# A graph-attention kernel on one core: batches of eight edge tiles in place of four

## The chip, the core and the metric

The kernel runs on one core of a Trainium2 chip. The metric is the device time of one execution in microseconds; the median of three is given. The core has TensorE (PE, its weight loads shown apart as PEld), VectorE (DVE), ScalarE (ACT), GpSimd (POOL) and SyncE (SP), each with an instruction queue of its own that it works off in order. Transfers run on 16 DMA engines; here SP and POOL issue nearly all of them.

## What is computed

One layer of graph attention over 6250 nodes with 128 features (8 heads of 16) and 206250 edges that are sorted by destination, then a residual and a layernorm. Cut to what matters:

```python
Qh, Kh, Vh = (h @ WQ), (h @ WK), (h @ WV)           # reshaped to (N, 8, 16)
Eh = (edge_attr @ WE)                               # (E, 8, 16)
score = einsum('ehd,ehd,ehd->eh', Kh[src], Qh[dst], Eh) / sqrt(16)
score = exp(clip(score, -5.0, 5.0))
msg = Vh[src] * score[:, :, None]
wV = segment_sum(msg, dst); Z = segment_sum(score, dst)
out = layernorm(x + wV / (Z + 1e-06))
```

## The kernel before

Edges are cut into 1612 tiles of 128 (one edge a partition), and tiles into batches of B = 4 (L26; the last eight tiles go in smaller ones, L45 to L53). One pass over the batches does everything.

Ahead of the pass, K and V of all nodes are computed (table, L216) and stored in device memory as kv, 1 KB a node. For each tile, POOL then issues one indirect DMA (gather, L293, issued at L300) that brings the 128 rows of kv that the edges' sources name into kvrows. The first XB = 12 batches don't wait for kv: they gather rows of x and are projected on PE (project, L305). kvrows has GB = 19 buffers of a batch each.

Q[dst] needs no gather, since the edges are sorted. Q's rows are computed 128 nodes at a time, split into three bf16 parts (q_rows, L245) and stored in device memory (qs, L255). For each batch, SP loads the slice qw of QW = 32 nodes, 96 rows (load_q, L258), at an offset read into a register. A transposed one-hot matrix onehotT, made by DVE from relb (each edge's row in the slice, loaded by L274), picks each edge's row in a matmul into the PSUM tile qps (L340). The edge features, loaded as ea in chunks of eight tiles (L284), are projected into the PSUM tile eps (L337). eps and qps have two buffers of one bank each.

The order is written out by hand in the loop at L433. In iteration b:

- loads by SP; the gather of batch b; its matmuls into eps and qps (stage_a, L329)
- DVE's products of batch b-1: kvrows by qps (L346), that by eps (L348), the sum over each head (L351), the clamp (L354) (stage_b)
- DVE's messages of batch b-2 (L382)
- DVE's one-hots of batch b+2, onehot (L322) and onehotT (L326) (stage_0)
- ACT's two exponentials of batch b-1 (weigh, L357)
- PE's sums of batch b-2, onehot by messages, into agg (stage_c, L400)

fill() puts one of the layernorm's 16 small DVE instructions between those. Finished blocks of 128 nodes are added up on PE (finish, L373), normalized and stored by SP. At the end of an iteration Q's rows for later batches are computed and at once stored (L473).

A count (count_inside, L187) makes sure that every edge's destination lies in the windows; if one doesn't, the program branches to a slow general version (any_order, L485).

## Time and profile before

| | |
|---|---|
| median of three executions | 2774.44 us (2774.24 to 2778.11) |
| the profiled execution's own time | 2045.27 us |
| its span | 2043.4 us |
| mean granted TensorE clock | 0.817 |
| instructions in the profile | 29203 |
| moved by DMA | 389.47 MB, mean 191 GB/s |

The profiled execution is 729 us shorter than the median of the others, and both are given here as they were measured. A line of a group reads: source line, engine, operation, what is written and read, shapes, number, then busy time and mean ns of one, then idle time of the engine just before them and what ended it. "issue" means that the engine waited for nothing that the profile shows. A table by stages gives, for each window of time, each engine's busy time and number of instructions. A timeline gives start, duration and, in brackets, the idle time before.

### The profile page before, as it was taken

To read this page: it belongs to the slowest core of one execution; us is meant where nothing else is said; L and a number is where in the kernel's file an instruction comes from. 1 tells how busy PE (TensorE), PEld (TensorE's weight loads), DVE (VectorE), ACT (ScalarE), POOL (GpSimd) and SP (SyncE) were. 2 spreads that over 40 slices of the span, in tenths; PEclk is the share of its full clock that TensorE was granted. 3 is DMA by queue.
4 is the path that set the end of the run, shared out by engine and by line. 5 is a ranking of instruction groups with operands and counts; after the bars stand their busy time and mean duration, and the time that the engine had idled before them with its cause. 6 is when DMAs were issued, how large, how long until landed. Compare 5 with 4: busy or idle time off the path is not lost.

```text
span 2043.4 us, 29203 instructions
## 1 busy us (share of the span) xinstructions
PE 1323.9 (65%) x8886; PEld 1239.0 (61%) x8886; DVE 1608.4 (79%) x3789; ACT 244.2 (12%) x1166; POOL 1531.9 (75%) x1619
## 2 busy tenths in 40 slices
PE   6957666666676666665676666665766666666664
PEld 5846666665566666565565566555665556656554
DVE  3789899988787777877778777778777878777777
ACT  2411111111111010111001111111011101111001
POOL 7777777777777777777777777777777777777774
PEclk9987887888778887878878787878688778787888
DMA  8776676675666566656756676667665676567662
GB/s 288 220 219 188 186 218 184 199 209 170 207 193 191 171 201 188 186 171 187 213 176 185 175 213 185 188 171 204 185 186 171 197 207 185 172 182 205 185 184 78
DMA packets 204560, 389.47 MB, mean 191 GB/s; under 512 B 80748, under 2 KB 107017, under 8 KB 204396
## 3 DMA queue, kind: packets, MB, share of 16 engines
q0 software_dynamic: 76592, 208.18, 35.9%
q1 hardware_dynamic: 126408, 178.67, 28.9%
q8 instruction: 73, 1.20, 0.2%
q10 hardware_dynamic: 1396, 0.67, 0.1%
q14 instruction: 91, 0.75, 0.1%
HBM read 372.55 MB, written 14.81 MB: 190 GB/s over the span
## 4 chain that ended last, share of the span: by engine, by line
DVE 30%; DMA 27%; POOL 20%; issue 15%; PE 5%; ACT 1%; SPq 1%; DVEq 0%; ACTq 0%; POOLq 0%
DMA kvrows<-kv,src 22%; POOL kvrows L300 20%; DVE kq L346 7%; DVE kq L348 6%; DVE sc L351 5%; DVE msg L382 3%; PE agg L400 3%; DMA relb<-relD 2%; DVE onehot L322 2%; DVE onehotT L326 2%; DVE sc L354 1%; DMA kv<-kvst 1%; PE kvps L316 1%; PE eps L337 1%; DVE w L581 1%
## 5 line engine op out<-in xcount | busy, mean ns | idle before, releaser
L300 POOL DMA_INDIRECT kvrows<-kv,src x1564 | 1485.2, 950 | 476.6 <-issue 387.0
L400 PE MATMUL agg<-msg,onehot 128*128 128x136 f32 x3224 | 606.7, 344 | 684.2 <-DVE msg L382 544.6
L400 PEld LDWEIGHTS agg<-msg,onehot 128*128 128x128 f32 x3224 | 519.3, 237 | 745.7 <-issue 712.1
L337 PE MATMUL eps<-we_sb,ea 128*128 128x128 f32 x3224 | 553.4, 329 | 1.9 <-DMA ea<-eaT 1.9
L337 PEld LDWEIGHTS eps<-we_sb,ea 128*128 128x128 f32 x3224 | 525.7, 245 | 2.9 <-ACT msg L362 2.1
L346 DVE TENSOR_TENSOR kq<-kvrows,qps 128x512 f32<-128x512 f32 x406 | 274.5, 676 | 205.7 <-DMA kvrows<-kv,src 177.2
L351 DVE TENSOR_REDUCE sc<-kq 128x32 f32<-128x512 f32 x406 | 276.5, 681 | 9.0
L348 DVE TENSOR_TENSOR kq<-kq,eps 128x512 f32<-128x512 f32 x406 | 276.9, 682 | 7.3 <-PE eps L337 0.2
L382 DVE TENSOR_TENSOR msg<-kvrows,bank 128x512 f32<-128x512 f32 x406 | 274.4, 676 | 6.7 <-ACT bank L360 6.7
L322 DVE TENSOR_TENSOR onehot<-bank,dst_sb 128x512 f32<-128x512 f32 x406 | 275.3, 678 | 0.0
L360 ACT ACTIVATE bank<-sc 128x32 f32<-128x32 f32 x406 | 81.7, 201 | 1505.6 <-DVE onehot L322 1490.2
L326 DVE TENSOR_SCALAR onehotT<-relb,node 96x512 bf16<-96x512 bf16 x406 | 146.1, 360 | 85.6 <-DMA relb<-relD 85.1
L340 PE MATMUL qps<-qw,onehotT 96*128 96x128 bf16 x1612 | 182.9, 244 | 0.0
L340 PEld LDWEIGHTS <-onehotT 96*128 96x128 bf16 x1612 | 148.7, 113 | 11.0
L354 DVE TENSOR_SCALAR sc<-sc 128x32 f32<-128x32 f32 x406 | 83.1, 205 | 9.0
L362 ACT ACTIVATE msg<-sc 128x32 f32<-128x32 f32 x406 | 86.5, 213 | 0.6
L370 PE MATMUL finps<-sum,shift 128*128 128x136 f32 x478 | 70.5, 297 | 0.0
L370 PEld LDWEIGHTS finps<-sum,shift 128*128 128x128 f32 x478 | 63.8, 204 | 0.0
L300 POOL DMA_INDIRECT kvrows<-x,src x48 | 45.7, 953 | 16.4 <-issue 14.0
L252 DVE TENSOR_TENSOR qr<-qrows,qst 128x128 f32<-128x128 f32 (+1 forms) x49 | 14.3, 291 | 49.8 <-ACT qst L251 49.8
L410 ACT COPY sum<-agg 128x136 f32<-128x136 f32 x146 | 38.8, 266 | 44.4 <-PE agg L400 43.1
L222 PE MATMUL kvacc<-wkv_sb,xT_sb 128*128 128x256 f32 (+1 forms) x98 | 29.3, 455 | 15.4 <-ACT kvst L227 6.0
(63 smaller groups left out, 397.4 us busy)
## 6 DMA issues: line engine op xcount, KB each, us to landing
ea<-eaT SPq DMA_DIRECT2D x201, 512.0 KB
relb<-relD SPq DMA_DIRECT2D x201, 192.0 KB
kvrows<-kv,src POOLq DMA_INDIRECT x1564
qw<-qs SPq DMA_DIRECT2D x403, 24.0 KB
kv<-kvst SPq DMA_DIRECT2D x12, 512.0 KB
qs<-qst SPq DMA_DIRECT2D x48, 96.0 KB
xb<-x SPq DMA_DIRECT2D x48, 64.0 KB
out<-h SPq DMA_DIRECT2D x48, 64.0 KB
```

The costliest lines, as they stand in the source:

```text
L300: nc.gpsimd.indirect_dma_start(out=g[:k, i, :f], out_offset=None, in_=rows, in_offset=bass.IndirectOffsetOnAxis(ap=src_col(t)[:k], axis=0))
L322: nc.vector.tensor_tensor(oh[:, :n], iota_p[:, None, :].to_broadcast([P, n, P]), rel[:, t0:t0 + n, None].to_broadcast([P, n, P]), op=ALU.i ...
L326: nc.vector.tensor_scalar(ohT[:, :n * P], rels[t0 // CH][:, e0:e0 + n * P], node[:QROWS], None, op0=ALU.is_equal)
L337: nc.tensor.matmul(pe[:, i, :], ea_tile(t0 + i), we_sb, start=True, stop=True)
L340: nc.tensor.matmul(pq[:, i, :], ohT[:, i * P:i * P + P], loaded[t0 // B], start=True, stop=True)
L346: nc.vector.tensor_tensor(t1[:, :n], g[:, :n, :D], pq[:, :n], op=ALU.mult)
L348: nc.vector.tensor_tensor(t1[:, :n], t1[:, :n], pe[:, :n], op=ALU.mult)
L351: nc.vector.tensor_reduce(sc[:, :n], t1[:, :n].rearrange("p b (h d) -> p b h d", h=H), axis=AX.X, op=ALU.add)
L354: nc.vector.tensor_scalar(sc[:, :n], sc[:, :n], -20.0, 20.0, op0=ALU.max, op1=ALU.min)
L370: nc.tensor.matmul(ps, shift[:, P - s:2 * P - s], sums[k], start=i == 0, stop=stop and i == len(parts) - 1)
L382: nc.vector.tensor_tensor(m[:, :n, :D].rearrange("p b (h d) -> p b h d", h=H), g[:, :n, D:].rearrange("p b (h d) -> p b h d", h=H), exp_p[ ...
L400: nc.tensor.matmul(aggs[k], oh[:, i, :], m[:, i, :], start=first and not final, stop=last)
```

## The change

Batches are of eight tiles (B = 8), so that the products, the reduction, the messages and both one-hots are one instruction for eight tiles. eps and qps become tiles of two PSUM banks with one buffer each; in an iteration, qps is filled first. A slice of Q is loaded for each eight tiles and holds QW = 42 nodes, 126 rows. scores(b-1) stands ahead of the matmuls of batch b; messages and sums of b-1 come in the same iteration as its scores, behind the one-hots of b+1. Q's rows are computed in one iteration and their store is issued in a later one (store_q). kvrows has 8 buffers of eight tiles. The table's copies from PSUM take four blocks at once. The tail is cut 4, 2, 2, 2, 1, 1. The functions stage_0, stage_a, stage_b and stage_c are renamed, and stage_0 is in two.

Left out below are the sizes of three buffers in the preparation (dB_sb and relq, one buffer in place of two) and unchanged lines between the parts.

```diff
@@ -23,21 +23,21 @@
 MW = D + H
-B = 4
-CH = 8
-GB = 19
-XB = 12
-TAIL = 8
+B = 8
+CH = B
+GB = 8
+XB = 6
+TAIL = 12
 HEAD = 132
 NG = (NT + G - 1) // G
-AHEAD = 2
 EB = 6
 SLAG = 2
-NJ = NT // B
-QW = 32
+NJ = (NT + B - 1) // B
+QW = 42
 QP = 3
 QROWS = QP * QW
-QLOOK = 6
+QLOOK = 3
+QLAG = 4
 QREG = 16
@@ -45,9 +45,9 @@
     while t < NT:
-        k = B
-        if t >= NT - TAIL:
-            k = 2 if NT - t > 3 else 1
+        k = min(B, NT - TAIL - t)
+        if k <= 0:
+            k = 4 if NT - t > 8 else 2 if NT - t > 3 else 1
         out.append(range(t, t + k))
...
@@ -200,8 +200,8 @@
         sp = fast.enter_context(tc.tile_pool(name="sums", bufs=7))
-        psE = fast.enter_context(tc.tile_pool(name="psE", bufs=2, space=bass.MemoryType.PSUM))
-        psQ = fast.enter_context(tc.tile_pool(name="psQ", bufs=2, space=bass.MemoryType.PSUM))
+        psE = fast.enter_context(tc.tile_pool(name="psE", bufs=1, space=bass.MemoryType.PSUM))
+        psQ = fast.enter_context(tc.tile_pool(name="psQ", bufs=1, space=bass.MemoryType.PSUM))
         psT = fast.enter_context(tc.tile_pool(name="psT", bufs=1, space=bass.MemoryType.PSUM))
@@ -215,24 +215,14 @@
             st = wp.tile([P, KB, 2 * D], F32, name="kvst", bufs=2)
-            blocks = range(b0, min(NB, b0 + KB))
-            for b in blocks:
-                n = min(P, N - b * P)
-                ps = (psE, psQ)[b % 2].tile([P, 2 * D], F32, name="kvacc", tag=("eps", "qps")[b % 2])
-                nc.tensor.matmul(ps[:n], xT_sb[:, LEFT + b * P:LEFT + b * P + n], wkv_sb,
-                                 start=True, stop=True)
-                if b % 2:
-                    nc.vector.tensor_copy(st[:n, b - b0, :], ps[:n])
-                else:
-                    nc.scalar.copy(st[:n, b - b0, :], ps[:n])
-            full = [b for b in blocks if (b + 1) * P <= N]
-            if full:
-                nc.sync.dma_start(
-                    kv[b0 * P:(b0 + len(full)) * P].rearrange("(b p) f -> p b f", p=P),
-                    st[:, :len(full), :])
-            if len(full) < len(blocks):
-                b = blocks[-1]
-                nc.sync.dma_start(kv[b * P:N], st[:N - b * P, b - b0, :])
+            k, n = min(KB, NB - b0), min(P, N - b0 * P)
+            w = b0 // KB % 2
+            ps = (psE, psQ)[w].tile([P, KB, 2 * D], F32, name="kvacc", tag=("eps", "qps")[w])
+            for i in range(k):
+                c0 = LEFT + (b0 + i) * P
+                nc.tensor.matmul(ps[:n, i, :], xT_sb[:, c0:c0 + n], wkv_sb, start=True, stop=True)
+            (nc.vector.tensor_copy if w else nc.scalar.copy)(st[:n, :k, :], ps[:n, :k, :])
+            nc.sync.dma_start(kv[b0 * P:b0 * P + (k - 1) * P + n].rearrange("(b p) f -> p b f", p=n), st[:n, :k, :])
@@ -240,20 +230,23 @@
-        built, loaded, regs, rels = [], {}, [], {}
+        built, stored, loaded, regs, rels = [], [], {}, [], {}
             nc.tensor.matmul(ps[:n], xT_sb[:, LEFT + q * P:LEFT + q * P + n], wq_sb, start=True, stop=True)
-            st = wp.tile([P, QP, D], BF16, name="qst", bufs=1)
+            st = wp.tile([P, QP, D], BF16, name="qst", bufs=2)
             r1 = wp.tile([P, D], F32, name="qr1", bufs=1)
             nc.vector.tensor_tensor(st[:n, 2, :], r1[:n], st[:n, 1, :], op=ALU.subtract)
+            built.append((q, n, st))
+
+        def store_q(q, n, st):
             nc.sync.dma_start(qs[q * P * QP:(q * P + n) * QP].rearrange("(p s) f -> p s f", s=QP), st[:n])
-            built.append(q)
+            stored.append(q)
@@ -304,45 +297,51 @@
-            pt = psT.tile([P, B, P], F32, name="xtps", tag="oT")
-            for i in range(n):
-                nc.tensor.transpose(pt[:, i, :], g[:, i, :D], ident)
-            xgT = wp.tile([P, B, P], F32, name="xgT", tag="kq")
-            nc.scalar.copy(xgT[:, :n], pt[:, :n])
-            for i in range(0, n, 2):
-                k = min(2, n - i)
-                pk = (psE, psQ)[i // 2 % 2].tile([P, 2, 2 * D], F32, name="kvps", tag=("eps", "qps")[i // 2 % 2])
-                for j in range(k):
-                    nc.tensor.matmul(pk[:, j, :], xgT[:, i + j, :], wkv_sb, start=True, stop=True)
-                nc.scalar.copy(g[:, i:i + k, :], pk[:, :k, :])
-
-        def stage_0(b):
+            xgT = wp.tile([P, B, P], F32, name="xgT", tag="kq", bufs=2)
+            for h in range(0, n, KB):
+                pt = psT.tile([P, KB, P], F32, name="xtps", tag="oT")
+                for i in range(KB):
+                    nc.tensor.transpose(pt[:, i, :], g[:, h + i, :D], ident)
+                nc.scalar.copy(xgT[:, h:h + KB], pt)
+                w = h // KB % 2
+                pk = (psE, psQ)[w].tile([P, KB, 2 * D], F32, name="kvps", tag=("eps", "qps")[w])
+                for i in range(KB):
+                    nc.tensor.matmul(pk[:, i, :], xgT[:, h + i, :], wkv_sb, start=True, stop=True)
+                nc.scalar.copy(g[:, h:h + KB, :], pk)
+
+        def edge_rows(b):
+
             t0, n = batches[b][0], len(batches[b])
-            oh = wp.tile([P, B, P], F32, name="onehot", bufs=AHEAD + 4)
+            oh = wp.tile([P, B, P], F32, name="onehot", bufs=4)
             nc.vector.tensor_tensor(oh[:, :n], iota_p[:, None, :].to_broadcast([P, n, P]),
                                     rel[:, t0:t0 + n, None].to_broadcast([P, n, P]), op=ALU.is_equal)
-            ohT = wp.tile([QROWS, B * P], BF16, name="onehotT", bufs=AHEAD + 2)
+            st8[b] = [n, oh]
+
+        def edge_columns(b):
+            t0, n = batches[b][0], len(batches[b])
+            ohT = wp.tile([QROWS, B * P], BF16, name="onehotT")
             e0 = t0 % CH * P
                                     op0=ALU.is_equal)
-            st8[b] = oh, ohT
-
-        def stage_a(b, g):
-            t0, n = batches[b][0], len(batches[b])
+            st8[b].append(ohT)
+
+        def expand(b, g):
+
+            t0 = batches[b][0]
+            n, oh, ohT = st8[b]
             if b < XB:
                 project(g, n)
-            oh, ohT = st8.pop(b)
+            pq = psQ.tile([P, B, D], F32, name="qps")
+            for i in range(n):
+                nc.tensor.matmul(pq[:, i, :], ohT[:, i * P:i * P + P], loaded[t0 // B], start=True, stop=True)
             pe = psE.tile([P, B, D], F32, name="eps")
                 nc.tensor.matmul(pe[:, i, :], ea_tile(t0 + i), we_sb, start=True, stop=True)
-            pq = psQ.tile([P, B, D], F32, name="qps")
-            for i in range(n):
-                nc.tensor.matmul(pq[:, i, :], ohT[:, i * P:i * P + P], loaded[t0 // B], start=True, stop=True)
             st8[b] = [n, g, oh, pe, pq]
-        def stage_b(b):
+        def scores(b):
             n, g, oh, pe, pq = st8[b]
-            t1 = wp.tile([P, B, D], F32, name="kq")
+            t1 = wp.tile([P, B, D], F32, name="kq", bufs=2)
             nc.vector.tensor_tensor(t1[:, :n], g[:, :n, :D], pq[:, :n], op=ALU.mult)
@@ -358,7 +357,7 @@
             nc.scalar.activation(exp_p[:, :n], sc[:, :n], AF.Exp, scale=0.25)
-            m = wp.tile([P, B, MW], F32, name="msg")
+            m = wp.tile([P, B, MW], F32, name="msg", bufs=2)
             nc.scalar.activation(m[:, :n, D:], sc[:, :n], AF.Exp, scale=0.25)
...
@@ -420,6 +419,7 @@
             q_rows(q)
+            store_q(*built[q])
         load_rel(0)
@@ -430,7 +430,7 @@
         held = []
-        for b in range(nbat + 3):
+        for b in range(nbat + 1):
             if b >= XB and not manual:
@@ -444,37 +444,45 @@
                     late_loads()
-                if b == min(XB + 8, nbat - 1):
+                if b == min(XB + 4, nbat - 1):
                     relative(C0, NT)
-                if b in (14, 18, 22):
-                    from_window(b // 4 - 2)
+                    for i in range(1, (NJ + P - 1) // P):
+                        from_window(i)
                 if b == 0:
-                    for i in range(AHEAD):
-                        stage_0(i)
-                stage_a(b, g)
+                    edge_rows(b)
+                    edge_columns(b)
+            if 0 <= b - 1 < nbat:
+                scores(b - 1)
+            if b < nbat:
+                expand(b, g)
             norms.extend(pending)
             ready.clear()
-            if 0 <= b - 1 < nbat:
-                stage_b(b - 1)
-            if 0 <= b - 2 < nbat:
-                messages(b - 2)
-            fill()
-            if b + AHEAD < nbat:
-                stage_0(b + AHEAD)
+            fill()
+            if b + 1 < nbat:
+                edge_rows(b + 1)
             if 0 <= b - 1 < nbat:
                 weigh(b - 1)
-            if 0 <= b - 2 < nbat:
-                stage_c(b - 2)
+            fill()
+            if b + 1 < nbat:
+                edge_columns(b + 1)
+            fill()
+            fill()
+            if 0 <= b - 1 < nbat:
+                messages(b - 1)
+                add_up(b - 1)
             fill()
             if b < nbat:
-                while len(built) < q_built(min(NJ - 1, batches[b][0] // B + QLOOK + 3)):
+                j = batches[b][0] // B + QLOOK
+                while len(stored) < q_built(min(NJ - 1, j + 1)):
+                    store_q(*built[len(stored)])
+                if len(built) < q_built(min(NJ - 1, j + QLAG)):
                     q_rows(len(built))
-            if b == min(60, nbat):
+            if b == min(30, nbat):
                 count_inside()
-            if b == min(80, nbat + 1):
+            if b == min(40, nbat):
                 inside = nc.values_load(cnt_i[0:1, 0:1], min_val=0, max_val=2 * EPAD,
@@ -604,7 +612,7 @@
         "dstT": np.ascontiguousarray(dstT.reshape(NT, P).T),
-        "dstB": dstT.reshape(NJ, B * P),
+        "dstB": np.concatenate([dstT, np.full(NJ * B * P - EPAD, -1, dst.dtype)]).reshape(NJ, B * P),
         "dst0": np.ascontiguousarray(dstT[None, ::B * P]),
```

More of the change, by code (lines that the diff above doesn't have):

```diff
@@ L119, in edge_attention @@
         ident = shift[:, P:2 * P]
-        dB_sb = [ip.tile([P, B * P], I32, name="dB_sb", bufs=2)]
+        dB_sb = [ip.tile([P, B * P], I32, name="dB_sb", bufs=1)]
         nc.scalar.dma_start(dB_sb[0][:min(P, NJ)], dstB[:min(P, NJ)])
@@ L151, in from_window @@
             if i == len(dB_sb):
-                dB_sb.append(ip.tile([P, B * P], I32, name="dB_sb", bufs=2))
+                dB_sb.append(ip.tile([P, B * P], I32, name="dB_sb", bufs=1))
                 nc.sync.dma_start(dB_sb[i][:k], dstB[a:a + k])
@@ L156, in from_window @@
             nc.vector.tensor_tensor(w[:k], d[:k, :1], bnd_c[:k, i:i + 1], op=ALU.min)
-            r = ip.tile([P, B * P], BF16, name="relq", bufs=2)
+            r = ip.tile([P, B * P], BF16, name="relq", bufs=1)
             nc.vector.tensor_scalar(r[:k], d[:k], w[:k], None, op0=ALU.subtract)
@@ L385, in messages, with add_up @@
                 exp_p[:, :n, :, None].to_broadcast([P, n, H, DH]), op=ALU.mult)
-        def stage_c(b):
+        def add_up(b):
             n, g, oh, m = st8.pop(b)
```

## The prediction

> **What bounds the kernel now.** I read the page's first and second parts, then the groups of part 5, then the timeline of POOL alone in the middle of the run, the table by stages, and last the waits.
>
> ```profile
> PE 1323.9 (65%) x8886; PEld 1239.0 (61%) x8886; DVE 1608.4 (79%) x3789; ACT 244.2 (12%) x1166; POOL 1531.9 (75%) x1619
> ```
>
> By busy time DVE leads, with 79%, and no engine is full. The groups correct that.
>
> ```profile
> L300 POOL DMA_INDIRECT kvrows<-kv,src x1564 | 1485.2, 950 | 476.6 <-issue 387.0
> ...
> L346 DVE TENSOR_TENSOR kq<-kvrows,qps 128x512 f32<-128x512 f32 x406 | 274.5, 676 | 205.7 <-DMA kvrows<-kv,src 177.2
> ```
>
> The gather on POOL has idle time in front of it, but nearly all of that is "issue": POOL waited for nothing. DVE's first product, in contrast, waits for gathered rows. The timeline of POOL alone:
>
> ```profile
> 1001.08 0.95 POOL L300 DMA_INDIRECT kvrows<-kv,src  x1 [0.30 <-issue]
> 1002.33 0.94 POOL L300 DMA_INDIRECT kvrows<-kv,src  x1 [0.30 <-issue]
> 1003.58 0.95 POOL L300 DMA_INDIRECT kvrows<-kv,src  x1 [0.30 <-issue]
> 1004.84 0.95 POOL L300 DMA_INDIRECT kvrows<-kv,src  x1 [0.30 <-issue]
> ```
>
> One gather every 1.250 us, 0.95 of work and 0.30 between two. The reader should check that this holds everywhere:
>
> ```profile
> 500.00:1000.00 500.00, 323.75 (x2137) 304.82 (x2136) 390.10 (x917) 52.72 (x270) 378.35 (x400) 0.79 0.64 188
> 1000.00:1500.00 500.00, 321.98 (x2147) 304.21 (x2148) 392.99 (x924) 52.86 (x273) 378.42 (x400) 0.80 0.64 187
> 1500.00:2000.00 500.00, 317.27 (x2139) 299.24 (x2137) 389.81 (x914) 51.43 (x268) 378.43 (x400) 0.81 0.65 188
> ```
>
> The columns are PE, PEld, DVE, ACT, POOL, clock, DMA share and GB/s: exactly 400 gathers in each 500 us. So 1612 gathers (1564 + 48) x 1.250 = 2015.0 us of the profiled execution's 2045.27; the other 30.3 are 3.7 before the first gather, some 18 after the last (2025.6 to 2043.4), and a few slips between. This execution is paced by POOL's queue of gathers, and DVE, at 3.95 us in a slot of 5.0 for four tiles, follows it.
>
> **How this stands to the median.** The median is 2774.44, 729 us over the profiled execution. Nothing on the page has that length. If all of it lay in the gathers, one would take (2774.44 - 30.3) / 1612 = 1.70 us; if it lay in batches, each of the 406 would carry 1.8 us more. The three times lie within 0.14% of each other, which speaks for one steady pacer, not for chance. I carry differences in us over to the median, and treat the unexplained 729 us as the main doubt.
>
> [...]128x256 takes 418 ns, 128x512 681 and 128x1024 1220 to 1224. [...]The steady 1.250 us shows no such stall here, whatever DVE does.[...]
>
> **The change, part by part.**
> Gathers: still 1612 on the same queue, first at the same place. Only the wait for a free buffer falls on every eighth instead of every fourth; the 0.30 before a gather is the same with or without it. Cost 0. Buffers fall from 19x4 = 76 tiles to 8x8 = 64. POOL has issued 37 tiles when DVE starts its first product at 50 us; tile 64 comes at 3.7 + 64 x 1.25 = 84 us, and the first batch should be released by about 70. No stall; 14 us in hand.
> DVE: for eight tiles, ten 512-wide instructions of 0.680 become five 1024-wide of 1.222: 6.80 - 6.11 = 0.69 us. onehotT: 2 x 0.361 becomes 0.361 + 512 x 0.355 ns = 0.54, the slope from 270 ns at 256 wide: 0.18. The clamp: 2 x 0.205 becomes 0.24: 0.17. Together 1.04 us, x 200 batches = 208 us. All of it lies beside POOL: it becomes more waiting for gathers.
> ACT: two exponentials of 0.21 for four tiles become two for eight, some 0.35 us saved, of an engine 12% busy: 0.
> PE: the same matmuls, 6987. At the granted clock eight tiles take (553 + 183 + 607 + 71) / 201.5 = 7.0 us of a slot of 10.0. What is new is one PSUM tile each for eps and qps in place of two. Behind qps's matmuls stand eps's and the sums in PE's queue. They begin when DVE has read the old tile; from the second product's end, eps needs 2.1 to 2.8 us, while DVE has the reduction, clamp, one-hots and messages, 1.22 + 0.24 + 1.22 + 0.54 + 1.22 = 4.4 us, before it wants them. 1.6 to 2.3 us in hand, so 0. If PE ran at half clock, its 5.6 us at full clock (eps 1.06, qps 0.39, agg 1.17 for four tiles, plus 0.4) would be 11.2 in a slot of 10.0: that cover would be gone, at 1.2 us a batch.
> Messages in their own iteration: the one-hots now lie between clamp and messages, and cover the exponential's 0.2 us. It shortens the way through the pipeline by a batch, which counts only at the end. There an eight-tile batch now stands ahead of the small ones; the last gather of it is 12 gathers, 15 us, from the end, and DVE's 7.5 + 4 + 11 us for it and the six small ones ends some 3 us later than before. Bounds: -2 to +4 us; if gathers take 1.70 us the cover is longer and it is 0. I take 0.
> Q's rows: SP waited 507 us in front of its stores of them (L255 for DVE's L254), and behind it stood relb, for which onehotT waited 85 us in 42 places. Storing late removes that, and so DVE stalls that POOL's pace hid anyway. qw loads fall from 403 to 202; relb grows from 192 to 252 KB for eight tiles. SP's queue is shorter: 0. The table's copies, four blocks at once, finish well ahead of 62.8 us, where the first gather of kv stands: the last store went out at 49.2.
> Sum: 0, between -2 and +4 us, on 2045.27; on the median 2774.
>
> **The rivals.**
> Same pace of gathers is my forecast (0.44): 2774, own range 2760 to 2785. What can be told from no change is 0.2%, 5.5 us.
> Faster (0.34): the 729 us that the page lacks are in DVE's and the hand-overs' time, which follow the number of batches. For it: DVE is the busiest by busy time, and 403 handshakes become 202. Against: nothing of it is seen, and the profiled pace is POOL's. All of DVE's 208 us gives 2566; half the slots, which I take, 2670.
> Slower (0.20): the transfers pace the unprofiled run. For eight tiles an engine moves ea 32 + kv 64 + relb 12 + qw 3 = 111 KB now[...]. It decides only when engines are busy nearly all the time; the page has 0.65.[...] Fewer 256-byte pieces of qw (38,700 to 25,500) speak against it.
> That the change doesn't do what it says (0.02): were a batch's nodes to span more than 42, the branch to the slow order would run, and add at least ten times the whole. A batch has 1024 of 206250 edges, 31 nodes of 6250 on average.
>
> **How the numbers follow.** From the forecast's 0.44, 0.26 lie within 0.2%, 0.11 below (fewer waits than I can see), 0.07 above (the end's extra batch). With 0.34 faster: 0.45. With 0.20 and 0.02 slower: 0.29. The range 2590 to 2850 takes in most of the faster case and half of the slower; some 0.16 is left out. The likeliest one's own range is above.
>
> **What would show it.** In the profile of the changed kernel: 80 gathers in each 100 us and a span of 2040 to 2048; DVE busy near 1400 us, with more waiting for kvrows; onehotT's wait for relb near zero; 128x1024 at 1.22 us. Wrong if POOL's gathers show gaps over 0.30 us that end with a DVE release, if kq waits for qps or eps by more than some 10 us in all, or if the times move by more than the span does: then the pacer of the unprofiled runs is another than the page's.

## The result: 3.1% slower, and a second level of time

The changed kernel took 2860.85 us (2853.72 to 2872.14, four executions) beside 2776.28 for the kernel before: a ratio of 1.0307, with a 95% interval from 1.0267 to 1.0347. The forecast was 2774. Both kernels were seen at two levels of time, a whole set of executions (taken together on one chip) at one or at the other: the kernel before near 2044 us as in its first profile, or near 2776 as in its times. One and the same chip showed both in different sets: for the kernel before, 2045.19 us in one and 2777.60 in another. The table has all comparisons of the two unchanged kernels.

| | kernel before | changed kernel | ratio |
|---|---|---|---|
| lower level, one execution each | 2043.81 | 2055.19 | 1.0056 |
| lower level, medians | 2045.19 | 2056.97 | 1.0048 (1.0032 to 1.0065) |
| upper level | 2776.28 | 2860.85 | 1.0307 (1.0267 to 1.0347) |

So there are two losses to explain: some 11 us at the lower level, and 84 us at the upper one. The profile after is of the upper level (span 2870.3 us), that of before shown above is of the lower one. First its busy times:

```profile
PE 1448.9 (50%) x8886; PEld 1324.2 (46%) x8886; DVE 1458.9 (51%) x2361; ACT 180.5 (6%) x736; POOL 1540.7 (54%) x1619
```

No engine is busy for more than 54% of the span; DVE works less than before, 1458.9 us in place of 1608.4. The groups of the profile after answer to the two shown of before, with three more of DVE:

```profile
L293 POOL DMA_INDIRECT kvrows<-kv,src x1564 | 1494.2, 955 | 1271.8 <-DVE msg L381 675.1
...
L345 DVE TENSOR_TENSOR kq<-kvrows,qps 128x1024 f32<-128x1024 f32 (+2 forms) x206 | 245.3, 1191 | 375.5 <-remote 206.0
L381 DVE TENSOR_TENSOR msg<-kvrows,bank 128x1024 f32<-128x1024 f32 (+2 forms) x206 | 246.2, 1195 | 293.6 <-ACT bank L359 280.7
L347 DVE TENSOR_TENSOR kq<-kq,eps 128x1024 f32<-128x1024 f32 (+2 forms) x206 | 246.8, 1198 | 253.5 <-remote 180.3
...
L242 DVE TENSOR_TENSOR qr<-qrows,qst 128x128 f32<-128x128 f32 (+1 forms) x49 | 14.3, 291 | 399.0 <-ACT qst L241 318.0
```

Over half of POOL's idle time, 675.1 us, ends with a release by DVE's messages: there all buffers for gathered rows were full, and POOL waited for DVE. The prediction had named such gaps as a sign that it is wrong. DVE in turn stood in front of both products and of the messages, and longest of all, 399.0 us in 49 places, in front of the arithmetic on Q's rows (L242), which needs PE's product and ACT's cast of it. "Remote" means that what ended the wait isn't among the records of this core; the products need gathered rows and PE's two tiles, and rows were no want while POOL stood with all buffers full. The table by stages (columns as before the change) has the pace:

```profile
500.00:1000.00 500.00, 256.60 (x1559) 235.18 (x1559) 265.48 (x427) 27.63 (x125) 271.15 (x284) 0.72 0.46 137
1000.00:1500.00 500.00, 239.46 (x1547) 221.38 (x1545) 252.31 (x401) 27.73 (x125) 274.76 (x288) 0.73 0.46 137
1500.00:2000.00 500.00, 242.26 (x1502) 224.79 (x1503) 250.91 (x403) 26.86 (x122) 272.15 (x286) 0.71 0.48 138
```

There are 284 to 288 gathers in each 500 us in place of 400, and the DMA share is 0.46 to 0.48 in place of 0.64: neither POOL nor the transfers set the pace. What PE does in such a stretch is seen in its timeline, here with DVE's and ACT's instructions of the same time:

```profile
978.38 3.69 PE L399 MATMUL agg<-msg,onehot 128*128 128x136 f32 x16 [2.85 <-issue]
...
986.92 0.27 PE L339 MATMUL eps<-we_sb,ea 128*128 128x128 f32 x1 [1.75 <-issue]
...
988.34 0.27 PE L339 MATMUL eps<-we_sb,ea 128*128 128x128 f32 x1 [1.16 <-issue]
...
990.47 0.37 PE L339 MATMUL eps<-we_sb,ea 128*128 128x128 f32 x1 [1.86 <-issue]
...
991.87 0.37 PE L339 MATMUL eps<-we_sb,ea 128*128 128x128 f32 x1 [1.03 <-issue]
...
992.58 0.58 PE L339 MATMUL eps<-we_sb,ea 128*128 128x128 f32 x1 [0.33 <-issue]
994.02 0.27 ACT L409 COPY sum<-agg 128x136 f32<-128x136 f32 x1 [17.41 <-PE eps L339]
...
994.19 0.23 ACT L359 ACTIVATE bank<-sc 128x64 f32<-128x64 f32 x1
...
994.45 1.22 DVE L381 TENSOR_TENSOR msg<-kvrows,bank 128x1024 f32<-128x1024 f32 x1 [8.44 <-ACT bank L359]
```

PE issues a matmul of eps every 0.7 to 2.1 us, and before each it waited for nothing that the profile shows. Over the whole profile such idle time of PE ("issue", gaps over 0.15 us) adds up to 731.7 us; in the lower-level profiles of the two kernels there is none. ACT's copy of a finished sum (L409) needs the sums (L399) that stand ahead of these matmuls in PE's queue. By their records, whose ends are modelled, they end at 982.07; the copy starts at 994.02, 11.95 us later and after 17.41 us of idle time. Behind it in ACT's queue stands the exponential (L359), which starts at 994.19, 0.17 us after the copy does, and for that DVE's messages (L381) waited 8.44 us. What makes PE late is not known. What follows from it is the subject of the experiments.

### The profile page after: what moved, and what is told of

The parts are those of the page before. It is cut to its first block, busy times and chain, and to the rows that moved or that the text cites. A ratio compares the mean times of both kernels' runs of the same rounds, so it can differ in the third digit from the quotient of the medians.

```text
span 2870.3 us, 26394 instructions
## 1 busy us (share of the span) xinstructions
PE 1448.9 (50%) x8886; PEld 1324.2 (46%) x8886; DVE 1458.9 (51%) x2361; ACT 180.5 (6%) x736; POOL 1540.7 (54%) x1619
## 5 line engine op out<-in xcount | busy, mean ns | idle before, releaser
L293 POOL DMA_INDIRECT kvrows<-kv,src x1564 | 1494.2, 955 | 1271.8 <-DVE msg L381 675.1
L399 PE MATMUL agg<-msg,onehot 128*128 128x136 f32 x3224 | 611.8, 356 | 433.2 <-DVE msg L381 225.1
L399 PEld LDWEIGHTS agg<-msg,onehot 128*128 128x128 f32 x3224 | 560.3, 256 | 496.9 <-issue 489.4
L345 DVE TENSOR_TENSOR kq<-kvrows,qps 128x1024 f32<-128x1024 f32 (+2 forms) x206 | 245.3, 1191 | 375.5 <-remote 206.0
L381 DVE TENSOR_TENSOR msg<-kvrows,bank 128x1024 f32<-128x1024 f32 (+2 forms) x206 | 246.2, 1195 | 293.6 <-ACT bank L359 280.7
L347 DVE TENSOR_TENSOR kq<-kq,eps 128x1024 f32<-128x1024 f32 (+2 forms) x206 | 246.8, 1198 | 253.5 <-remote 180.3
L336 PE MATMUL qps<-qw,onehotT 126*128 126x128 bf16 x1612 | 155.2, 248 | 359.7 <-DVE kq L345 323.1
L336 PEld LDWEIGHTS <-onehotT 126*128 126x128 bf16 x1612 | 133.8, 114 | 375.5 <-issue 369.5
L350 DVE TENSOR_REDUCE sc<-kq 128x64 f32<-128x1024 f32 (+2 forms) x206 | 246.5, 1196 | 3.7
L316 DVE TENSOR_TENSOR onehot<-bank,dst_sb 128x1024 f32<-128x1024 f32 (+2 forms) x206 | 245.8, 1193 | 0.0
L242 DVE TENSOR_TENSOR qr<-qrows,qst 128x128 f32<-128x128 f32 (+1 forms) x49 | 14.3, 291 | 399.0 <-ACT qst L241 318.0
L409 ACT COPY sum<-agg 128x136 f32<-128x136 f32 x146 | 39.8, 272 | 1253.4 <-remote 642.5
L324 DVE TENSOR_SCALAR onehotT<-relb,node 126x1024 bf16<-126x1024 bf16 (+2 forms) x206 | 95.9, 465 | 2.0 <-DMA relb<-relD 2.0
L359 ACT ACTIVATE bank<-sc 128x64 f32<-128x64 f32 (+2 forms) x206 | 47.1, 229 | 688.8 <-issue 443.1
L361 ACT ACTIVATE msg<-sc 128x64 f32<-128x64 f32 (+2 forms) x206 | 49.6, 241 | 0.0
```

Of the source, the lines that this page charges most:

```text
L293: nc.gpsimd.indirect_dma_start(out=g[:k, i, :f], out_offset=None, in_=rows, in_offset=bass.IndirectOffsetOnAxis(ap=src_col(t)[:k], axis=0))
L316: nc.vector.tensor_tensor(oh[:, :n], iota_p[:, None, :].to_broadcast([P, n, P]), rel[:, t0:t0 + n, None].to_broadcast([P, n, P]), op=ALU.i ...
L324: nc.vector.tensor_scalar(ohT[:, :n * P], rels[t0 // CH][:, e0:e0 + n * P], node[:QROWS], None, op0=ALU.is_equal)
L336: nc.tensor.matmul(pq[:, i, :], ohT[:, i * P:i * P + P], loaded[t0 // B], start=True, stop=True)
L345: nc.vector.tensor_tensor(t1[:, :n], g[:, :n, :D], pq[:, :n], op=ALU.mult)
L347: nc.vector.tensor_tensor(t1[:, :n], t1[:, :n], pe[:, :n], op=ALU.mult)
```

## The experiments

Three theories were written down. H, later called C: the changed kernel is coupled more tightly, so that late hand-overs from PE (its results reach the engine that waits for them late) get through to DVE and POOL. G: the gathers themselves are slower. T: transfers of 126 rows in place of 96 pace it, an estimate of the author's that no run shows. R is a cost that is the same everywhere, D one that has nothing to do with a late PE; S and F are told with their runs. Unless said otherwise, edits are to the changed kernel.

**Both kernels once more, unchanged.**

> The kernel before, unchanged: a second profile of it. Theory H (hand-overs from PE that arrive late, in bouts, set the time of nearly all executions; the profiled one shown before had none): span near 2774 us, DVE's and ACT's instructions that wait for PE start some 5 to 14 us after PE's last matmul in a part of the batches, and gathers on POOL no longer come every 1.25 us without a gap. Theory G (the gather itself takes longer in most executions, 1.70 us in place of 1.25): span near 2774, no late hand-over, a gather's duration or the pause before it longer throughout. Neither: the span is again 2045.

> The changed kernel, unchanged: whether the late hand-overs of its profile repeat. Theory H: span 2850 to 2875 us, about a third of ACT's sum copies start over 5 us after PE's last matmul of the group, some 1100 to 1200 us of such delays in all. Theory G: the delays are a mishap of one execution, and the span changes by over 5%.

Measured: 2043.67 and 2055.19 us, both at the lower level, with 80 gathers in each 100 us and no late hand-over. The 11.6 us between the spans (2041.8 and 2053.4) are in two places. The last gather starts at 2029.3 in place of 2023.2, after steps that are the same 1.250 us in the middle but longer in more places; and from there to the end it takes 24.0 us in place of 18.6 (the tail); 6.1 and 5.4 make 11.5. For the upper level this decided nothing.

**Messages and sums one iteration later.**

```diff
+            if 0 <= b - 2 < nbat:
+                messages(b - 2)
...
-            if 0 <= b - 1 < nbat:
-                messages(b - 1)
-                add_up(b - 1)
+            if 0 <= b - 2 < nbat:
+                add_up(b - 2)
```

The messages stand between clamp and one-hots then, the sums where they were, and the loop runs once more.

> The changed kernel with messages and sums of batch b-2, not b-1, in iteration b, as before the change. Theory H with coupling (the change is slower because fewer batches are in flight when a hand-over is late): 60 to 150 us faster than the changed kernel, 2700 to 2800. Theory H without coupling (the delays are the same whatever the depth): 2850 within 1%. Theory T[...]: 2850 within 1%.

Measured: 2055.18 us, against 2055.19 for the changed kernel. At the lower level no cost of the messages' place is seen, by one execution each: the last gather starts 2.7 us later, and the tail is 2.6 us shorter (21.4). The same kernel is timed again at the end.

**Slices of 128 rows, for T.**

```diff
-QROWS = QP * QW
+QROWS = 128
...
-                    min_val=0, max_val=(N - QW) * QP,
+                    min_val=0, max_val=(N - QW - 1) * QP,
...
-            np.array([min(N, P * q_built(j)) - QW for j in ...
+            np.array([min(N, P * q_built(j)) - QW - 1 for j in ...
```

> The changed kernel with slices of 128 rows in place of 126: the two extra rows match no edge[...]. Theory T[...]: 2774 or less, at least 60 us faster. Theory H: 2850 within 1%, since the DMA engines are busy 0.45 of the time in the changed kernel.

Measured: 52469.72 us. With the bound one lower the last node lies in no window, so the count falls short and the program takes the branch to the general order. Nothing follows for T from it; it does show the price of that branch, 50 ms. Against T stands the DMA share of 0.46 to 0.48 at the upper level.

**The changed kernel timed, and three single edits.**

> The changed kernel as it is, timed beside the kernel before. Theory C (the changed kernel is coupled more tightly: with one PSUM tile for eps and qps and the messages in the same iteration, whatever makes PE's hand-overs late reaches DVE and POOL): where the kernel before needs about 2044, this one needs 2053 to 2057 (+0.5%); where the kernel before needs about 2776, this one needs 2850 to 2870 (+3%). Theory R (a cost that is the same everywhere): the same difference in us, about +11, at either level.

Measured: 2056.97 us beside 2045.19, a ratio of 1.0048 (1.0032 to 1.0065). With 1.0307 at the upper level this is C's picture, not R's: 12 us at one level, 84 at the other.

Next the longer steps between gathers. These lines are from the timeline of the changed kernel at the lower level (its second profile, of 2055.19 us):

```profile
1372.21 0.95 POOL L293 DMA_INDIRECT kvrows<-kv,src  x1 [0.30 <-DVE sc L350]
...
1373.37 0.48 DVE L324 TENSOR_SCALAR onehotT<-relb,node 126x1024 bf16<-126x1024 bf16 x1
1373.46 1.20 POOL L293 DMA_INDIRECT kvrows<-kv,src  x1 [0.30 <-issue]
...
1374.97 0.95 POOL L293 DMA_INDIRECT kvrows<-kv,src  x1 [0.30 <-issue]
```

A gather that starts 0.09 us after onehotT takes 1.20 us in place of 0.95. Of the 64 gathers over 0.99 us in that profile 53 overlap an onehotT in time, of the other 1548 only 175. That is the ground of theory S: onehotT holds the gather up.

```diff
-            nc.vector.tensor_scalar(ohT[:, :n * P], rels[t0 // CH][:, e0:e0 + n * P], node[:QROWS], None,
-                                    op0=ALU.is_equal)
+            for c in range(0, n * P, 4 * P):
+                w = min(4 * P, n * P - c)
+                nc.vector.tensor_scalar(ohT[:, c:c + w], rels[t0 // CH][:, e0 + c:e0 + c + w], node[:QROWS], None,
+                                        op0=ALU.is_equal)
```

> The changed kernel with onehotT written by two instructions of 512 columns in place of one of 1024. Theory S (a gather that starts while DVE writes onehotT is held up until DVE is done; the longer instruction holds it longer, 0.25 us each): the gathers over 0.99 us that lie beside onehotT become shorter, the steps between gathers lose some 4 to 6 of the 12 us that they are over 1.250 each, and the time falls by 4 to 6 us against the changed kernel, 2049 to 2051 where the kernel before needs 2044. If the gathers are longer for another reason (more bytes of relb, fewer buffers): no difference beyond 1 us.

Measured: 2052.89 us. Its interval (1.0026 to 1.0054) overlaps that of the changed kernel, so the times alone don't separate them. The median is 4.1 us below the changed kernel's, as expected, but above the 2049 to 2051 named. The gathers are clearer: their excess (the sum of their times less 0.947 us for each) is 5.8 us, where the changed kernel had 12.1 in the same set and 9.4 before; the last gather starts at 2025.6 in place of 2031.9.

The tail is the other place. At its start stand these, from the same profile as the lines above:

```profile
2027.41 1.17 PE L339 MATMUL eps<-we_sb,ea 128*128 128x128 f32 x4
...
2028.38 1.39 PE L369 MATMUL finps<-sum,shift 128*128 128x136 f32 x10
...
2029.81 0.27 ACT L376 COPY fin<-finps 128x136 f32<-128x136 f32 x1 [4.36 <-PE finps L369]
2029.97 0.21 ACT L359 ACTIVATE bank<-sc 128x32 f32<-128x32 f32 x1
...
2030.21 0.69 DVE L381 TENSOR_TENSOR msg<-kvrows,bank 128x512 f32<-128x512 f32 x1 [4.07 <-ACT bank L359]
```

DVE's messages wait 4.07 us for the exponential, the exponential stands behind ACT's copy of a finished block (fin, L376), and that waits for PE's matmuls, which come behind eps of the next batch. That is theory F.

```diff
-            for q in ready:
-                finish(q)
-            ready.clear()
             fill()
             if b + 1 < nbat:
                 edge_rows(b + 1)
             if 0 <= b - 1 < nbat:
                 weigh(b - 1)
+            for q in ready:
+                finish(q)
+            ready.clear()
             fill()
```

> The changed kernel with ACT's copy of a finished block (fin) behind the two exponentials in place of ahead of them; PE's and DVE's orders stay. Theory F (the exponential of a batch waits behind fin, which waits for PE's matmuls of the next batch, and at the end DVE's messages wait 4.07 us for it): DVE's wait of msg for bank falls from 115 us to under 20, the tail behind the last gather shrinks from 24.0 to 19 to 21 us, and the time falls by 3 to 5 us at a level of 2044; at a level of 2776 it falls by 10 to 80 us, since the late hand-overs of PE reach DVE in fewer places. If the tail is set by the eight-tile batch itself: no difference.

Measured: 2052.35 us (ratio 1.0038, 1.0026 to 1.0050). DVE's wait of the messages for the exponential fell from 116.7 us to 2.8, and the tail from 24.0 to 21.7, where 19 to 21 was expected. The median fell by 4.6 us, within the expected 3 to 5, but by luck in good part: the gathers' excess fell too, from 12.1 to 7.1 us, which F doesn't say (perhaps because onehotT came to lie elsewhere among the gathers).

```diff
-        psE = fast.enter_context(tc.tile_pool(name="psE", bufs=2, space=bass.MemoryType.PSUM))
-        psQ = fast.enter_context(tc.tile_pool(name="psQ", bufs=2, space=bass.MemoryType.PSUM))
+        psE = fast.enter_context(tc.tile_pool(name="psE", bufs=1, space=bass.MemoryType.PSUM))
+        psQ = fast.enter_context(tc.tile_pool(name="psQ", bufs=1, space=bass.MemoryType.PSUM))
```

This one is an edit to the kernel before.

> The kernel before with one buffer each for eps and qps (of one bank) in place of two, nothing else. Theory C: at a level of 2044 within 4 us of the kernel before, since POOL's pace hides it; at a level of 2776 slower by 1 to 4%. Theory R, or the messages alone being the coupling: no difference at either level.

Measured: 2047.56 us, a ratio of 1.0011 (1.0002 to 1.0020), thus 2.4 us at the lower level, as C allows. PE's "issue" idle time, 0 in the kernel before at this level, is 163.5 us here, so such idle time alone doesn't make the upper level.

**Theory S by the instruction's form.** The same onehotT by a tensor_tensor, slower for DVE (1.22 us for 126x1024 in place of 0.48) but, so the thought, without what holds the gathers up:

```diff
-            nc.vector.tensor_scalar(ohT[:, :n * P], rels[t0 // CH][:, e0:e0 + n * P], node[:QROWS], None,
-                                    op0=ALU.is_equal)
+            nc.vector.tensor_tensor(ohT[:, :n * P], rels[t0 // CH][:, e0:e0 + n * P],
+                                    node[:QROWS].to_broadcast([QROWS, n * P]), op=ALU.is_equal)
```

> The changed kernel with onehotT written by a tensor_tensor against the broadcast node number in place of a tensor_scalar: the same values, at a slower rate (about 1.2 us for 126x1024 in place of 0.48). Theory S (DVE's fast two-byte tensor_scalar keeps POOL[...] until it ends): the gathers beside onehotT are no longer over 0.99 us (fewer than 15 such in the run, from 64 to 77), the gathers' excess over 0.947 us falls from 9 to 12 us to under 3, and the last gather starts 6 to 9 us earlier; 2047 to 2050 where the kernel before needs 2045, though DVE is busy 150 us longer. If the gathers are longer merely because DVE is at work, or for relb's bytes: no fewer, and the time is equal or longer.

Measured: 2131.03 us, 4.3% above the kernel before (2043.91): the expectation failed, the outcome is the one named for DVE merely being at work, and the gathers' excess rose to 84.4 us. The timeline shows how:

```profile
1304.85 1.22 DVE L324 TENSOR_TENSOR onehotT<-relb,node 126x1024 bf16<-126x1024 bf16 x1
...
1305.18 1.71 POOL L293 DMA_INDIRECT kvrows<-kv,src  x1 [0.30 <-DVE w L589]
...
1307.19 0.95 POOL L293 DMA_INDIRECT kvrows<-kv,src  x1 [0.30 <-issue]
```

The gather that starts inside onehotT ends at 1306.89, 0.82 us after onehotT does. Over the whole run it is the same: a gather that starts 0.4 to 0.5 us before onehotT's end takes 1.28 us in the mean, at 0.8 to 0.9 us 1.69, at 1.1 to 1.2 us 1.96; one that had begun before onehotT takes 0.946 in the median. That DVE is merely at work isn't it: 791 times a gather of the same run starts inside one of DVE's products, messages or onehot of 128x1024, which take 1.2 us as well but have one input in PSUM, and one of these gathers is over 0.99 us. So the holding up is real and lasts past the end of DVE's instruction (by 0.82 us in these lines), but not only the fast form, the tensor_scalar of 0.48 us, does it. One thing that sets this tensor_tensor apart from those 791 cases is that both of its inputs lie in SBUF. What lies behind that in the hardware no run here shows.

The last edit came with two others in one kernel: fin behind the exponentials as above, and

```diff
-TAIL = 12
+TAIL = 20
```

so that the end is cut 4, 4, 4, 2, 2, 2, 1, 1.

> The changed kernel with three edits: onehotT by tensor_tensor, fin behind the exponentials, and the last 20 tiles in batches of 4, 4, 4, 2, 2, 2, 1, 1 in place of 12 in 4, 2, 2, 2, 1, 1. If the 11 us are the sum of held-up gathers (6 to 9) and the longer tail (5.4), both are gone: 2041 to 2045 where the kernel before needs 2045, thus no slower than it. If something else holds the changed kernel back: it stays 4 us or more above the kernel before. At a level of 2776 a coupled PE would keep it above 2800.

Measured: 2120.47 us, so the expectation failed. The gathers' excess, 71.8 us, hides the rest; the tail came down to 19.4 us, against 23.3 with tensor_tensor alone and 18.6 in the kernel before.

**One operand in PSUM.** The "run before this one" is the kernel with onehotT by tensor_tensor alone; the diff is against that.

```diff
-        bank = psX.tile([P, P + B * H], F32, name="bank")
+        bank = psX.tile([P, P + B * H + 1], F32, name="bank")
...
+        node_p = bank[:, P + B * H:]
+        nc.vector.tensor_copy(node_p, node)
...
-                                    node[:QROWS].to_broadcast([QROWS, n * P]), op=ALU.is_equal)
+                                    node_p[:QROWS].to_broadcast([QROWS, n * P]), op=ALU.is_equal)
```

> The run before this one with the node number that onehotT is compared with kept in PSUM in place of SBUF; the instruction stays a tensor_tensor of about 1.2 us. Theory S2 (what holds a gather up is a DVE instruction that takes two streams from SBUF, or its fast two-byte form; a gather that starts inside one ends 0.8 us after that one's end): with one operand in PSUM no gather beside onehotT is long, the gathers' excess falls from 84 us to under 3, the last gather starts at 2020 to 2023, the tail stays 23 to 24, 2046 to 2049 where the kernel before needs 2044. If the length of DVE's instruction alone decides: 2125 to 2135 again.

Measured: this set ran at the upper level, 3014.43 us beside 2776.44, so the times expected don't apply. The gathers do:

```profile
1264.75 1.22 DVE L326 TENSOR_TENSOR onehotT<-relb,bank 126x1024 bf16<-126x1024 bf16 x1 [0.23 <-ACT bank L361]
1265.09 0.95 POOL L295 DMA_INDIRECT kvrows<-kv,src  x1 [0.30 <-issue]
```

Same instruction, same 1.22 us, one operand in PSUM, and the gather inside it takes 0.95 us. Of 82 gathers that start inside an onehotT none is long (0.948 in the mean), and the excess is 3.1 us. The level isn't the reason: the changed kernel's profile at the upper level has 89 gathers that start inside its onehotT, and 77 of them take over 0.99 us. That is S2. The 9% are another matter, and not taken apart: DVE is busy 158 us longer than in the changed kernel (1617.1 and 1458.9) at a level where nothing hides it, and since onehotT now reads the tile that ACT's exponentials are written to, the wait for them moved from the messages to onehotT (304.5 us in 108 places).

> The kernel of three edits with the node number in PSUM: fin behind the exponentials, last 20 tiles in smaller batches, onehotT by tensor_tensor from PSUM. The tail was 19.4 us with these edits; with the gathers free the sum is 3.4 + 1611 x 1.2506 + 3 + 19.4 = 2040.5 us of span, 2041 to 2044 by the time, 0 to 3 us below the kernel before. If the eight-tile batches cost something else on the way: above 2046.

Measured: 2952.39 us, also at the upper level, 62 us less than without fin's move and the smaller batches at the end; some 10 us of these are the tail (45.5 and 35.6). Which of the two edits brought the rest isn't separated. Above 2800 it is as a coupled PE demands. As a version to beat the kernel before it failed.

**A load on PE.** To see which part exposes the kernel, four kernels got the same extra work, each matmul into eps issued twice:

```diff
                 nc.tensor.matmul(pe[:, i, :], ea_tile(t0 + i), we_sb, start=True, stop=True)
+                nc.tensor.matmul(pe[:, i, :], ea_tile(t0 + i), we_sb, start=True, stop=True)
```

> The kernel before with every matmul into eps issued twice (the second writes the same values over the first), which adds 3224 matmul instructions, some 530 us of PE's time, to make PE late by known means. Theory C (the changed kernel is more exposed to a late PE): this one stays POOL-paced or nearly, 2044 to 2120, and the changed kernel with the same load loses 3% or more against it. Theory D (the exposure is the same and the loss of 3% has another cause): both within 1% of each other.

> The changed kernel with every matmul into eps issued twice. Theory C: 3% or more above the kernel before with the same load (2150 to 2350 where that one takes 2044 to 2120), with POOL waiting for msg and DVE's products for qps and eps. Theory D: within 1% of it.

> The kernel before with one PSUM tile each for eps and qps and every matmul into eps issued twice. If the single tiles are what exposes the changed kernel: as slow as the changed kernel with the load, within 1%, or slower. If it is the longer batch or finish: within 1% of the kernel before with the load.

> The changed kernel with fin behind the exponentials and every matmul into eps issued twice. If the exponential that waits behind fin, and so behind PE's matmuls of the next batch, is what exposes the changed kernel: at least half of its loss against the kernel before with the load is gone. If it is the single tiles: less than a quarter.

Measured, all in one set at the upper level (kernel before without the load: 2746.22):

| with the load | us |
|---|---|
| kernel before | 2831.35 |
| changed kernel | 3084.18 |
| kernel before, one PSUM tile each | 2835.04 |
| changed kernel, fin behind the exponentials | 3066.07 |

The changed kernel stands 8.9% above the kernel before with the same load (3084.18 / 2831.35), as C says. Single PSUM tiles take 1.0013 of the kernel before's time: in its order they aren't it. Fin's move gives back 18 of 253 us, 7%: it isn't either, and that says more. The messages' wait for the exponential fell by it from 211.2 to 5.2 us, yet DVE's idle time only from 1631.5 to 1605.9: the wait in front of Q's rows grew from 496.6 to 645.6. A wait for late PE that is taken away in one place comes back in another. The messages' place was not tried under this load. The absolute times expected were those of the lower level and don't apply.

**The last two: the kernel before at the upper level, and the messages again.**

> The kernel before, unchanged, for its profile. If it takes 2740 to 2790 again: theory C wants late hand-overs here too, so that PE's and ACT's waits show 'remote' and 'issue' in the hundreds of us and POOL waits for msg, in all some 700 us, a smaller share for each tile than the changed kernel's. If POOL is paced by gathers of more than 1.25 us each instead, theory G (the gathers themselves are slower) is right. If it takes 2044, it shows nothing new.

Measured: 2776.11 us, and so the profile that was missing:

```profile
L300 POOL DMA_INDIRECT kvrows<-kv,src x1564 | 1480.6, 947 | 1160.3 <-DVE msg L382 446.9
...
L346 DVE TENSOR_TENSOR kq<-kvrows,qps 128x512 f32<-128x512 f32 x406 | 274.2, 675 | 702.1 <-remote 529.9
...
L382 DVE TENSOR_TENSOR msg<-kvrows,bank 128x512 f32<-128x512 f32 x406 | 274.6, 676 | 54.3 <-ACT bank L360 52.5
L348 DVE TENSOR_TENSOR kq<-kq,eps 128x512 f32<-128x512 f32 x406 | 277.1, 682 | 17.0 <-remote 9.9
```

The gathers take the same 947 ns: G is out. POOL waits for DVE here as well. DVE stands 702.1 us in front of its first product, where it stood 219.2 at the lower level, and now for PE or "remote", not for rows. The messages wait 54.3 us, and the second product 17.0. DVE's busy time is that of the first profile (1600.7 and 1608.4 us), its idle time grew from 435.0 to 1173.6. So the 729 us between the first profile and the median lie in hand-overs, in this kernel too, and PE's are the ones seen to be late; PE's "issue" idle time is 354.4 us here.

> The changed kernel with messages and sums of a batch one iteration later, as the kernel before had them (b-2), nothing else. Where the kernel before takes 2740 to 2790: if the messages' place is what exposes the changed kernel, the ratio falls from 1.031 to 1.005 or less; if the longer batch itself does, it stays at 1.02 or more. Where the kernel before takes 2044: 2054 to 2057, as in the single look before.

Measured: 2788.55 us beside 2777.60, a ratio of 1.0048 (1.0017 to 1.0079), against 1.0307 for the changed kernel. One edit, the place of messages and sums, takes away 72 of the 84 us. (The changed kernel's 2860.85 is from another set, with the kernel before at 2776.28.) What is left, 11 us, is as much as the changed kernel loses at the lower level. The profile shows where the wait was:

```profile
L347 DVE TENSOR_TENSOR kq<-kq,eps 128x1024 f32<-128x1024 f32 (+2 forms) x206 | 246.7, 1198 | 610.2 <-remote 567.4
...
L345 DVE TENSOR_TENSOR kq<-kvrows,qps 128x1024 f32<-128x1024 f32 (+2 forms) x206 | 245.9, 1193 | 163.6 <-remote 94.2
L381 DVE TENSOR_TENSOR msg<-kvrows,bank 128x1024 f32<-128x1024 f32 (+2 forms) x206 | 245.2, 1190 | 90.2 <-ACT bank L359 82.3
```

DVE's idle time in front of these groups, in the three profiles at the upper level (us):

| | kernel before | changed | messages later |
|---|---|---|---|
| first product | 702.1 | 375.5 | 163.6 |
| second product | 17.0 | 253.5 | 610.2 |
| messages | 54.3 | 293.6 | 90.2 |
| Q's rows | 164.3 | 399.0 | 306.5 |
| all of DVE's (span less busy time) | 1173.6 | 1411.4 | 1329.2 |

With messages later the two products wait longer (773.8 in place of 629.0), since a late PE still shows there, but messages and Q's rows less, and the span is 72.5 us shorter (2797.8 and 2870.3). PE's wait for messages in front of its sums, 225.1 us in the changed kernel, is 7.0. PE was no better in that execution: its "issue" idle time is 790.6 us (731.7 in the changed kernel), so the gain isn't that of a quieter execution.

## Why the prediction was wrong, step by step

- **"Messages in their own iteration"**, taken at 0, is the step that failed. It says that the one-hots lie between clamp and messages and "cover the exponential's 0.2 us". They cover 0.2 us, but not a late PE. With messages of b-2 a late result had an iteration to pass. With messages of b-1 it goes within one iteration from PE through ACT's queue, where the copy of the last batch's sum and fin stand ahead of the exponential, to DVE's messages, and from these to PE's sums, behind which Q's rows stand. At the upper level the place of messages and sums costs 72 us of the 84. At the lower level no cost is seen (2055.18 and 2055.19), and from that level's profile alone it was priced. That this place costs the 72 us is shown; which link of the chain carries them is not. The wait for the exponential alone does not, going by the runs with the load: nearly all of it went there with fin's move, and 7% of the loss came back.
- **"How this stands to the median"** carried differences in us from a profile of 2045 to a median of 2774. It named the 729 us as the main doubt, and then summed as if they were a constant. They are waiting time that depends on how the engines are coupled.
- **"Faster"** placed the 729 us rightly, in hand-overs, and priced them wrongly: it let half of them go with the number of handshakes. DVE's busy time did fall, from 1600.7 to 1458.9 us at the upper level, and its idle time rose from 1173.6 to 1411.4 (span less busy time).
- **"Slower", by transfers**, had the side right, but by luck: nothing paced by the DMA engines was seen, at a share of 0.46 to 0.48 of them, and most of the loss went with the messages' place while the slices stayed at 126 rows. Whether transfers of 126 rows cost more than those of 96 was not tested.
- **"Gathers ... Cost 0"** was off by 6 to 9 us at the lower level. The prediction took the steady step of 1.250 us as showing that no gather is held up, whatever DVE does. The step is steady in the middle; most of the few long gathers are where onehotT is, 3.1 us of excess in the kernel before and 9.4 to 12.1 with an onehotT of 0.48 us in place of 0.36.
- **The end**, "-2 to +4 us" with 0 taken and "some 3 us later" named, measured 5.4 us (24.0 less 18.6). The exponential behind fin, 2.3 us of it by fin's move, was not in it.
- **PE and PSUM**, 0 with 1.6 to 2.3 us in hand: right for the kernel before, where single tiles cost 2.4 us at the lower level and nothing that can be told under load at the upper. The count of matmuls, 6987, stands in no view; PE has 8886 instructions before and after, which bears out that they are the same. Two buffers of the eight-tile size were not tried.
- **DVE's 208 us hidden beside POOL**: right at the lower level. The groups fall by about as much (five 1024-wide groups of 246 us in place of five 512-wide of 274 to 277, onehotT 144.2 to 99.8, clamp 85.1 to 47.2, together some 230), 128x1024 took 1.22, and the wait for gathered rows grew from 196.7 to 222.5 us. Busy time fell by 142 only, as instructions overlap at their ends (in the second profile of the changed kernel the clamp of 1372.13 lasts 0.20 us, and onehot starts at 1372.24) and the groups count that time twice, so the 1400 named was too low.
- **Q's rows**: onehotT's wait for relb fell from 76.6 to 4.8 us and brought nothing, as said. But the part was priced by SP's queue alone. DVE's wait for ACT's cast of the rows grew from 48.6 to 151.8 us at the lower level, where POOL's pace hides it, and from 164.3 to 399.0 at the upper, as much as the messages' wait. No run moves this part by itself, so what it adds to the 84 us stays open. (The first gather of kv starts at 64.06 us, not at 62.8, which is the last of x; nothing hangs on it.)

What stays open is why PE issues so slowly in whole sets of runs and not in others of the same kernel on the same chip. No run here separates a cause. Nor was the changed kernel without the load seen in more than one set at the upper level. That the longer batch loses in waiting what it saves in DVE's work (busy 132 us less than the kernel before, and yet no faster, in the last run) is seen, but not taken apart. The kernel that the runs point to, messages later, fin behind the exponentials, the smaller batches at the end and onehotT in halves, was not run.

## What to carry to other kernels

When a profile and the median lie apart by a quarter, the sum made on the profile is a sum for another regime: ask for each part of the change what it costs if one engine's results arrive 10 us late, and treat as suspect each step that brings an engine's result into the iteration that uses it. A wait is priced by all that stands ahead of the awaited instruction in its queue, not by its own 0.2 us; and a wait taken away is not yet time gained, as it may come back in front of the next instruction. Beside a queue of gathers that paces a kernel, look not only at the median gather but at the long ones, and at what DVE runs under them.

## What was not expected of the hardware

- A gather that starts while DVE runs onehotT, as a tensor_tensor with two inputs in SBUF or as the tensor_scalar, ends about 0.82 us after that instruction does (it takes 1.71 us in place of 0.95 in the lines shown of the one, and 1.20 in those of the other); with one input in PSUM it takes 0.948 us in the mean of 82.
- The same kernel takes 2045.19 or 2777.60 us, on one chip, in different sets of executions. At the upper level PE issues matmuls singly, 0.7 to 2.1 us apart in the lines shown, and ACT's copies of sums wait up to 21.6 us; the gathers keep their 0.95 us.
- PE's granted clock is lower at the upper level (0.725 in place of 0.818 for the kernel before), but it doesn't make the level: the kernel before with one PSUM tile each and the load had 0.820 there, and took as long as the one with two tiles at 0.761. In the stretch shown the clock was 1.00 from 982 to 988 us, where PE's gap of 1.75 us lies.
